# Another order of a graph layer's first loads and last stages, and 358 picked tiles in place of 355

## The chip, the cores and the metric

The kernel runs on one core of a Trainium2 chip. A core has five engines with an instruction queue each, which run side by side and wait for each other by semaphores: TensorE (PE in the profile; its weight loads are PEld), VectorE (DVE), ScalarE (ACT), GpSimd (POOL) and SyncE (SP). SP, ACT and POOL also issue DMA transfers. The metric is the device time of one execution in microseconds; the median of three runs before the change is 1521.2 us (1520.66 to 1521.42). One further execution was profiled.

## The reference, cut to what matters

200,000 edges, sorted by destination, carry messages between 6,250 nodes with 64 features (E edges; `src`, `dst` are node numbers):

```python
w     = silu(edge_attr @ W1 + b1) @ W2 + b2                     # E x 9
h_src = x[src]                                                  # E x 64: a row per edge
msg   = einsum('ef,em,fmg->eg', h_src, edge_sh * w, W_tp)
agg   = segment_sum(msg, dst, 6250) / sqrt(16)
emb   = silu(c_noise[:, None] @ Wn1 + bn1) @ Wn2 + bn2
gamma, beta = split(emb, 2)
out   = layernorm(x + agg * (1 + gamma) + beta)
```

The costly line is `x[src]`: 200,000 rows of 256 bytes in random order.

## The kernel before, in words

**Tiles and groups.** 128 edges are a tile; 16 tiles are a group (`KB`); there are 98 groups (`NBLK`), numbered from 0, of which the last has 11 tiles. The source rows of a group lie in a buffer `hs[g]` (128 x 16 x 64); there are seven such buffers. A row of `x` gets there in one of three ways:

- *Gather* (`gather`, L91): POOL issues an indirect DMA per tile. Group g's gathers stand in POOL's queue six groups ahead (`AHEAD`).
- *Pick* (`pick`, L475 to L486): for the last `picked(g)` tiles of a group, three or four, TensorE multiplies a one-hot matrix with all of `x`, kept in SBUF as two halves `xs[0]`, `xs[1]` (a rounded value and the rest). That is 7 x 2 matmuls into `px`; VectorE masks the result (`xm`, L484) and reduces it into `hs` (L486). The one-hot operands `hot_k` are made by `hots` (VectorE, L460) from keys that stand in every partition (`pk`, copied by ScalarE in `keys` from `kr`, a broadcast load).
- *Direct row loads* (`load_rows`, L106): for every sixth group from 7 on (`SPG`), tile 0 is loaded row by row by SP.

So a group has 16 - `picked(g)` gathers, one fewer if it is in `SPG`. In the kernel before, `picked` is 3 for g mod 8 in {0, 3, 6}, else 4: 355 picks and 1192 gathers.

**Stages of a group.** `hidden` (L403, L411) is the first layer of the edge network with its Silu, `second` (L420) the second, `weights` (L430 to L442) turns the result and multiplies it by `sh` and the one-hot windows `oh` (from `near`, L382) into `a`. `windows` (L504 to L514) sums each tile's messages into windows of 8 nodes: 16 pairs of matmuls of `hs` and `a` into `pz`, which ScalarE copies into `zt`. `project` (L538, L543) multiplies two groups' `zt` by `W_tp`; `turn`, `halves` and `place` (L549, L524 to L528, L559) put the window sums at their nodes; `bring` (L576) and `finish` (L670 to L684) end 128-node blocks with the layer norm and a store.

**Order.** The order is written out by hand: each engine's queue is the order in which the Python code calls. The main loop, for i in 0..97, calls gather(i+6), the loads, `pick(i+1, 0)` with the node stages of i woven between its matmuls, `hidden(i+2)`, `second(i+1)`, `windows(i)`, `project` for odd i, and then picks 1 to 3 of group i+1 (L603 to L651). At the end (i = 96, 97) `windows` came after the picks; then the last projection.

**Setup** (`setup`, L134 to L321) loads the operands, issues the gathers of groups 0 to 5, makes all keys with VectorE (nine passes over 392 columns, L205 to L225), sends them to DRAM and reads them back into every partition (`kd`, `kr`), and splits `x`: ScalarE copies each of seven slices once to PSUM and once, rounded, to `xs[0]`; VectorE subtracts (L294). Then the first picks.

Of the kernel before, what the change touches and what calls it, by code (L numbers as in the profile page):

```python
# [15 lines left out]
P = 128  # L16
N, F, M, D, H, E = 6250, 64, 9, 32, 64, 200000
NJ = 49
# [31 lines left out]
def picked(g):  # L50

    return Q - (3 * g % 8 < 3)
# [7 lines left out]
def gnn_resnorm_kernel(ctx: ExitStack, tc: tile.TileContext, x, src, dst, dst_row, ea, sh, cn,  # L60
# [18 lines left out]
    with ExitStack() as fast:  # L79
# [54 lines left out]
        def setup(temp):  # L134
# [4 lines left out]
            for q in range(4):  # L139
                nc.sync.dma_start(w1bd[q * D:(q + 1) * D, (q % 2) * H:(q % 2 + 1) * H], w1)  # L140
            nc.sync.dma_start(src_i[:, AHEAD * KB:], src[:, AHEAD * KB:])
            xb_r = xb.rearrange("p j f -> p (j f)")
            row_i = xb_r[0:1, 0:NBLK * KB].bitcast(I32)
            nc.scalar.dma_start(row_i, dst[0:1, :])
            first_i = temp.tile([NBLK, KB], I32)
            nc.scalar.dma_start(first_i, dst[0].rearrange("(g k) -> g k", k=KB))
            cn_j = temp.tile([NJ, P], F32)
            nc.scalar.dma_start(cn_j, cn)
            for s in range(2):
                nc.scalar.dma_start(b1c[s * H:(s + 1) * H, :], b1.unsqueeze(1))  # L150
# [3 lines left out]
            for h0, h1 in ((0, 2), (2, 4), (4, 7)):  # L154
                nc.scalar.dma_start(xk[:, h0:h1, :], x_v[:, h0:h1, :])
            load(0)
            for s in range(2):
                nc.sync.dma_start(w2p[s * H:(s + 1) * H, s * M:(s + 1) * M], w2)
            nc.sync.dma_start(dst_i, dst)
# [14 lines left out]
            one = temp.tile([1, 1], F32)  # L174
            nc.vector.memset(one, 0.0)
            one_o = temp.tile([1, 1], F32)
            nc.scalar.activation(one_o, one, AF.Silu)
            row_f = xb_r[0:1, NBLK * KB:2 * NBLK * KB]
            nc.scalar.copy(row_f, row_i)
            first_t = temp.tile([NBLK, KB], F32)  # L180
            nc.scalar.copy(first_t, first_i)
# [5 lines left out]
            nc.vector.tensor_add(ident2, ident[:, 0:F], ident[:, F:P])  # L187
            zero = temp.tile([P, 1], F32)
            nc.vector.memset(zero, 0.0)
            for k in range(2):  # L190
                nc.vector.memset(ht[k][H:H + 1], 1.0)
            nc.vector.memset(wtc2[F:P, 4], 0.0)
            ones1 = temp.tile([1, P], F32)
            nc.vector.memset(ones1, 1.0)
            nc.vector.memset(eps, EPS)
            nc.vector.tensor_copy(nk, nk_i)
            nc.vector.tensor_copy(wi, n_i[:, 0:W])
            nc.vector.tensor_copy(li, n_i[:, 0:J])


            zt_r = zt.rearrange("p a c k w -> p (a c k w)")
            s_f, kp, kh, rest, t0, t1 = [zt_r[:, k * C:(k + 1) * C] for k in range(6)]
            ti = [t.bitcast(I32) for t in (t0, t1)]
            s_f = s_f.rearrange("p (g k) -> p g k", k=Q)
            nc.vector.tensor_copy(s_f[:, 0:NBLK - 1, :],  # L205
                                  src_i.rearrange("p (g k) -> p g k", k=KB)[:, 0:NBLK - 1, KB - Q:])
            nc.vector.tensor_copy(s_f[:, NBLK - 1, :], src_i[:, NT - Q:NT])
            s_f = s_f.rearrange("p g k -> p (g k)")
            nc.vector.tensor_scalar(ti[0], s_f, 2675.0, None, op0=ALU.mult)
            nc.vector.tensor_scalar(ti[0], ti[0], 17, None, op0=ALU.logical_shift_right)  # L210
            nc.vector.tensor_copy(kp, ti[0])
            nc.vector.scalar_tensor_tensor(rest, kp, -float(J * J), s_f, op0=ALU.mult, op1=ALU.add)
            nc.vector.tensor_scalar(ti[1], rest, 37.0, None, op0=ALU.mult)
            nc.vector.tensor_scalar(ti[1], ti[1], 8, None, op0=ALU.logical_shift_right)
            nc.vector.tensor_scalar(kh, ti[1], float(P), None, op0=ALU.mult)
            kf = s_f
            nc.vector.tensor_add(kf, kp, kh)
            for c0 in range(0, C, P):
                n = min(P, C - c0)
                p_kt = psum.tile([P, P], F32, tag=("s", "r")[c0 // P % 2], name=f"p_kt{c0}")  # L220
                nc.tensor.transpose(p_kt[0:n], kf[:, c0:c0 + n], ident)
                kt = t1[:, c0 // 2:c0 // 2 + P // 2].bitcast(F16)
                nc.scalar.copy(kt[0:n], p_kt[0:n])
                nc.sync.dma_start(kd[c0:c0 + n, :], kt[0:n])
            nc.vector.scalar_tensor_tensor(jl, kh, -float(J) / P, rest, op0=ALU.mult, op1=ALU.add)  # L225
            hidden(0, act=False)
            load_keys(0)
            load_keys(LB)
            for c in range(KB // 4):
                for s in range(2):  # L230
                    q = c * D + s * M
                    nc.sync.dma_start(b2c[q:q + M, :], b2.unsqueeze(1))


            rel_v = rel.rearrange("p (a b c) -> p a b c", a=2, b=2)
            dst_v = dst_i.rearrange("p (a b c) -> p a b c", a=2, b=2)
            row_v = row_f.rearrange("p (a b c) -> p a b c", a=2, b=2)

            def base(a_):
                p_b = psum.tile([P, 2, KB * P // 4], F32, tag="p1", name=f"p_b{a_}")  # L240
                for b_ in range(2):
                    nc.tensor.matmul(p_b[:, b_, 0:NBLK * KB // 4], ones1, row_v[:, a_, b_, :], start=True, stop=True)
                nc.vector.tensor_sub(rel_v[:, a_], dst_v[:, a_], p_b[:, :, 0:NBLK * KB // 4])


# [8 lines left out]
            nc.vector.tensor_copy(pw, pw_i)  # L254

            def ids():
                p_nid = psum.tile([P, NBLK], F32, tag="s", name="p_nid")
                nc.tensor.matmul(p_nid, sel, first_f, start=True, stop=True)
                nc.vector.scalar_tensor_tensor(nid, p_nid, pw, lo, op0=ALU.add, op1=ALU.subtract)

            def between(h):

                if h == 0:
                    p_f = psum.tile([KB, NBLK], F32, tag="s", name="p_f")
                    nc.tensor.matmul(p_f, first_t, ident[0:NBLK, 0:NBLK], start=True, stop=True)
                    nc.scalar.copy(first_f, p_f)
                elif h == 1:
                    keys(0)
                    hots(0, 0, Q)
                elif h == 3:  # L270
                    p_cn = psum.tile([P, NJ], F32, tag="s", name="p_cn")
                    nc.tensor.matmul(p_cn, cn_j, ident[0:NJ, 0:NJ], start=True, stop=True)
                    cn_s = temp.tile([P, NJ], F32)
                    nc.scalar.copy(cn_s, p_cn)
                    nc.sync.dma_start(cn_d, cn_s)
                    nc.sync.dma_start(wn1c, wn1.rearrange("o h -> h o"))
                    nc.sync.dma_start(bn1c, bn1.unsqueeze(1))
                    gate_load(0)
                    nc.sync.dma_start(wn2a[0:H, :], wn2)
                    nc.sync.dma_start(wn2a[H:H + 1, :], bn2.unsqueeze(0))  # L280
                    for q in range(2):
                        n = (M + 1 - q) // 2
                        nc.sync.dma_start(wtc2[q * F:(q + 1) * F, 0:n, :], wtp[:, q:M:2, :])
                    load(LB)
                    with nc.allow_non_contiguous_dma(reason="2048 words, once"):
                        nc.sync.dma_start(src_r, src[:, SPG[0] * KB:NBLK * KB:6 * KB].rearrange("p g -> g p"))


            for h in range(J):
                xh = gam[:, h * J:(h + 1) * J, :].rearrange("p l f -> p f l")  # L290
                xp = psum.tile([P, F, J], F32, tag="px" if h in (2, 3) else "pz", name=f"x{h}", bufs=2)
                nc.scalar.copy(xp, xh)
                nc.scalar.copy(xs[0][:, h], xh)
                nc.vector.tensor_sub(xs[1][:, h], xp, xs[0][:, h].bitcast(F32))  # L294
                if h == 1:
                    hidden_act(0)
                between(h)
            pick(0, 0)
            keys(1)
            hots(1, 0, Q)  # L300
            base(0)
            near(0)
            second(0)
            pick(0, 1)
            base(1)

            nc.vector.memset(rel[:, NT:], 0.0)
            if E % P:
                nc.vector.memset(rel[E % P:, NT - 1:NT], 0.0)
            for f in weights(0):  # L310
                f()
            ids()
            hidden(1)
            nc.scalar.copy(zt[F:P, :, 4].rearrange("p a k w -> p a (k w)"),
                           zero[F:P, :, None].to_broadcast([F, 4, P]))
# [543 lines left out]
```

## Time and profile before

| | |
|---|---|
| median of three runs | 1521.2 us |
| the profiled execution's own time | 1521.78 us |
| its span, first to last instruction | 1519.9 us |
| mean granted TensorE clock | 0.983 of full speed |
| PE busy | 1438.0 us (95%) |
| POOL busy | 1129.3 us (74%) |
| VectorE busy | 1135.4 us (75%) |
| ScalarE busy | 526.1 us (35%) |
| gathers (L91) | 1192, 946 ns each |
| pick matmuls (L475) | 4970 recorded, 1090.6 us busy |

What lies around the span is 1521.78 - 1519.9 = 1.88 us. Busy time counts an engine's instructions alone: issuing a DMA or waiting at a semaphore is not busy, and for POOL's gathers some time between two of them is not either. A row of the groups gives line, engine, operation, what it writes and reads, the count, busy time and mean, then the engine's idle time ahead of them and what ended it. The timeline gives start, length, and in brackets the idle time before.

### The profile page before, as it was taken

The page shows a single profiled execution, that of the slowest core. Times are in us where ns is not written, and L with a number is a line of the kernel's source. Part 1 is how long each engine was busy: PE and PEld are TensorE (multiplying, and loading weights), DVE is VectorE, ACT ScalarE, POOL GpSimd, SP SyncE. Part 2 cuts the span into 40 slices and gives each one's busy share as a digit, 9 for nine tenths or more (in the row PEclk, how much of TensorE's full clock was granted, in tenths as well). Part 3 has the DMA queues.
Part 4 walks back from the last instruction along what each step waited for, and adds up shares of the span by engine and source line. Part 5 has one row for each costly group of instructions (what it writes and reads, how often), then busy time and mean ns, then how long its engine had stood idle before and what let it go on. Part 6 is the DMA issues. An engine that isn't in the chain of part 4 may idle for free.

```text
span 1519.9 us, 34363 instructions
## 1 busy us (share of the span) xinstructions
PE 1438.0 (95%) x10810; PEld 1192.7 (78%) x10810; DVE 1135.4 (75%) x1987; ACT 526.1 (35%) x1335; POOL 1129.3 (74%) x1201
## 2 busy tenths in 40 slices
PE   4998999999999999999999999989998998999995
PEld 2787888888888788888888888878777887878784
DVE  5686777877877878777777877768677777687773
ACT  4223342433423333332423424424233333333331
POOL 7777777777777777777777777777777777777772
PEclk9999999999999999999999999999999999999997
DMA  6422232222222222222322222222222222222210
GB/s 171 95 56 63 54 76 53 64 59 70 65 56 72 58 63 71 60 63 54 74 59 55 72 52 63 71 54 61 53 72 53 59 55 71 52 55 59 73 29 15
DMA packets 90939, 96.16 MB, mean 63 GB/s; under 512 B 37161, under 2 KB 51451, under 8 KB 90748
## 3 DMA queue, kind: packets, MB, share of 16 engines
q0 software_dynamic: 38144, 39.14, 13.4%
q1 hardware_dynamic: 51842, 53.09, 12.1%
q8 instruction: 88, 1.44, 0.4%
q10 hardware_dynamic: 762, 1.64, 0.3%
q14 instruction: 103, 0.84, 0.2%
HBM read 92.04 MB, written 1.73 MB: 62 GB/s over the span
## 4 chain that ended last, share of the span: by engine, by line
PE 57%; POOL 18%; issue 9%; SPq 5%; DMA 5%; DVE 4%; ACT 2%; DVEq 0%; POOLq 0%; ACTq 0%
PE px L475 41%; POOL hs L91 18%; PE pz L504 5%; DMA hs<-in_x_dram,src_i 4%; PE p L403 3%; SPq L106 3%; PE pt L543 3%; PE p L420 2%; SPq L101 2%; PE p L430 1%; PE ps L559 1%; PE ps L589 0%; ACT st L411 0%; DVE hot_k L460 0%; DVE xm L484 0%
## 5 line engine op out<-in xcount | busy, mean ns | idle before, releaser
L91 POOL DMA_INDIRECT hs<-in_x_dram,src_i x1192 | 1128.0, 946 | 364.3 <-issue 330.7
L475 PE MATMUL px<-xs,hot_k 128*128 128x448 f32 x4970 | 1090.6, 372 | 9.4 <-DVE xs L294 8.8
L475 PEld LDWEIGHTS px<-xs,hot_k 128*128 128x128 f32 x4970 | 896.8, 189 | 93.9 <-issue 10.9
L484 DVE SCALAR_TENSOR_TENSOR xm<-li,jl,px 128x448 f32<-128x448 f32 x355 | 240.3, 677 | 203.6 <-PE px L475 202.0
L460 DVE TENSOR_TENSOR hot_k<-pk,nk 128x896 fp32r<-128x896 f32 x355 | 370.6, 1082 | 3.1 <-ACT pk L454 3.1
L411 ACT ACTIVATE st<-p,b1c 128x1024 f32<-128x1024 f32 x98 | 109.5, 1118 | 405.4 <-PE p L403 405.1
L486 DVE TENSOR_REDUCE hs<-xm 128x64 f32<-128x448 f32 x355 | 220.1, 620 | 12.2
L514 ACT COPY zt<-pz 64x160 f32<-64x160 f32 (+2 forms) x784 | 213.5, 272 | 40.6 <-PE pz L504 28.0
L504 PEld LDWEIGHTS pz<-a,hs 128*64 128x64 f32 x3126 | 110.2, 142 | 68.1 <-issue 61.2
L504 PE MATMUL pz<-a,hs 128*64 128x72 f32 x3126 | 124.6, 234 | 27.0 <-DMA hs<-in_x_dram,src_i 11.5
L442 DVE TENSOR_TENSOR a<-oh,p 128x1152 f32<-128x1152 f32 x98 | 132.7, 1354 | 3.3
L436 DVE TENSOR_TENSOR p<-p,sh 128x72 f32<-128x72 f32 x196 | 47.0, 240 | 100.9 <-ACT rt L546 45.2
L403 PE MATMUL p<-ea,w1bd 64*128 64x512 f32 x392 | 113.3, 655 | 0.0
L565 ACT COPY carry<-ps 128x128 f32<-128x128 f32 x48 | 12.8, 266 | 273.4 <-PE ps L559 273.4
L420 PEld LDWEIGHTS p<-st,w2p 128*32 128x32 f32 x784 | 15.8, 108 | 83.2 <-issue 39.0
L420 PE MATMUL p<-st,w2p 128*32 128x256 f32 x784 | 63.5, 396 | 7.8 <-DVE xb L356 7.8
L680 ACT ACTIVATE var<-var,eps 128x2 f32<-128x2 f32 (+1 forms) x25 | 7.4, 295 | 179.2 <-DVE var L679 179.2
L543 PE MATMUL pt<-zt,wtc 128*64 128x128 f32 x960 | 64.3, 281 | 2.6 <-ACT zt L514 1.7
L543 PEld LDWEIGHTS pt<-zt,wtc 128*64 128x64 f32 x960 | 55.0, 142 | 3.8 <-ACT zt L514 1.9
L454 ACT CAST pk<-kr 128x384 f32<-128x384 f16 (+1 forms) x98 | 53.8, 549 | 2.2 <-DMA kr<-kd 2.2
L430 PE MATMUL p<-ident,p2s 128*128 128x128 f32 x196 | 53.3, 273 | 0.0
L403 PEld LDWEIGHTS p<-ea,w1bd 64*128 64x128 f32 x392 | 30.0, 187 | 28.7 <-issue 28.0
(122 smaller groups left out, 529.0 us busy)
## 6 DMA issues: line engine op xcount, KB each, us to landing
hs<-in_x_dram SPq DMA_DIRECT2D x2048, 0.2 KB
ea<-in_ea_dram SPq DMA_DIRECT2D x49, 512.0 KB
hs<-in_x_dram,src_i POOLq DMA_INDIRECT x1192
kr<-kd SPq DMA_DIRECT2D x49, 256.0 KB
sh<-in_sh_dram SPq DMA_DIRECT2D x49, 144.0 KB
cb<-cn_d SPq DMA_DIRECT2D x12, 128.0 KB
out_dram<-o SPq DMA_DIRECT2D x24, 64.0 KB
gam<-in_x_dram ACTq DMA_DIRECT2D x2, 448.0 KB
```

Source lines behind the costliest of these rows:

```text
L91: hs_dma[g] = [nc.gpsimd.indirect_dma_start(out=hs[g][:, t - g * KB, :], out_offset=None, in_=x, in_offset=bass.IndirectOffsetOnAxis(ap=sr ...
L403: nc.tensor.matmul(p1[:, i, :], w1bd[i * 64:(i + 1) * 64, :], e[i * 64:(i + 1) * 64, :], start=True, stop=True)
L411: nc.scalar.activation(st[g], p1_t.pop(g), AF.Silu, bias=b1c)
L420: nc.tensor.matmul(p2[g][c * D:(c + 1) * D, 0, :].rearrange("p (i e) -> p i e", i=2), w2p, s[:, :, c * P:(c + 1) * P], start=True, stop=True)
L442: nc.vector.tensor_mul(a[g], oh_t.pop(g)[:, :, None, :].to_broadcast([P, KB, M, W]), sw.unsqueeze(3).to_broadcast([P, KB, M, W]))
L460: nc.vector.tensor_tensor(hot_k[g, t], pk_t[g][:, t, None, :].to_broadcast([P, J, P]), nk.unsqueeze(2).to_broadcast([P, J, P]), op=ALU.is_ ...
L475: nc.tensor.matmul(px.rearrange("p f l -> p (f l)"), hot_k[g, t][:, h, :], xs[i][:, h].rearrange("p f l -> p (f l)"), start=(h == 0 and i ...
L484: nc.vector.scalar_tensor_tensor(xm, li[:, None, :].to_broadcast([P, F, J]), jl[:, c:c + 1], px, op0=ALU.is_equal, op1=ALU.mult)
L486: nc.vector.tensor_reduce(hs[g][:, tiles(g) - q + t, :], xm, AX.X, ALU.add)
L504: mm = nc.tensor.matmul(pz[v * F:(v + 1) * F, k // 2].rearrange("p m w -> p (m w)"), hsg[:, k0 + k, :], ag[:, k0 + k].rearrange("p m w -> ...
L514: nc.scalar.copy(z[h * F:(h + 1) * F, 0:5 - h, k0 + v:k0 + n:2, :].rearrange("p m k w -> p k m w"), pz[v * F:(v + 1) * F, 0:(n + 1 - v) // ...
L543: nc.tensor.matmul(pt[h * F:(h + 1) * F, 0, 0:P], wtc2[:, c, :], z[h][:, c], start=(c == 0), stop=(c == 4))
```

## The change

- `picked` is 3 for g mod 3 = 0 and for the last group, else 4: 358 picks, 1189 gathers. The last group has 3 picks and 7 gathers where it had 4 and 6.
- Setup: ScalarE's queue issues only the loads of `x`, ahead of everything; SP's queue has the rest in the order of first use (the source indices stay SP's first). Keys of groups 0 and 1 alone are made first; they are spread over the partitions by a matmul of ones with a diagonal matrix (`keys_first`) in place of the way through DRAM; the other groups' keys follow later (`keys_rest`). `x` is split from SBUF: ScalarE copies once, VectorE subtracts with both operands in SBUF. The first layer of group 0 comes behind the first pick. The first node of each tile, `row_i`, is loaded by DMA into every partition, so that `rel` is a subtraction of two SBUF operands in place of matmuls of ones and a subtraction from PSUM.
- End: `windows(96)` stands behind the first pick of group 97, with `project(48)` between picks and `place` behind the last; `bring` of blocks 46 and 47 comes before `windows(97)`, whose second half is done first and whose copies are shared by ScalarE and VectorE. PSUM tags change.
- Stores are issued by a list that the next iteration empties. In SP's queue they stand where they stood.

The diff, cut:

```diff
 def picked(g):
-    return Q - (3 * g % 8 < 3)
+    return Q - (g % 3 == 0 or g == NBLK - 1)
...
+            x_v = x.rearrange("(p h l) f -> p h (l f)", h=J, l=J)
+            for h0, h1 in ((0, 1), (1, 2), (2, 4), (4, 7)):
+                nc.scalar.dma_start(xk[:, h0:h1, :], x_v[:, h0:h1, :])
...
+            load(0, split=True)
+            nc.sync.dma_start(dst_i[:, 0:2 * KB], dst[:, 0:2 * KB])
+            nc.sync.dma_start(row_i[:, 0:2 * KB], rows(dst[0, 0:2 * KB], P))
...
+            def keys_first(g, kf, tag):
+                pk_t[g] = psum.tile([P, Q, P], F32, tag=tag, name=f"pk{g}")
+                for t in range(picked(g)):
...
+                    nc.vector.tensor_scalar(dg, ident, kf[:, c:c + 1], None, op0=ALU.mult)
+                    nc.tensor.matmul(pk_t[g][:, t, :], ones, dg, start=True, stop=True)
...
+            def split(h):
+                xh = gam[:, h * J:(h + 1) * J, :].rearrange("p l f -> p f l")
+                nc.scalar.copy(xs[0][:, h], xh)
+                nc.vector.tensor_sub(xs[1][:, h], xh, xs[0][:, h].bitcast(F32))
+            kf = keys_of(0, LB)
+            keys_first(0, kf, "r")
+            hots(0, 0, 1)
+            for h in range(J):
+                split(h)
+                if h == J // 2:
+                    hots(0, 1, 2)
...
+            pick(0, 0)
+            hots(0, 2, Q)
+            hidden(0)
+            keys_first(1, kf, "s")
...
+            nc.sync.dma_start(dst_i[:, 2 * KB:], dst[:, 2 * KB:])
+            nc.sync.dma_start(row_i[:, 2 * KB:], rows(dst[0, 2 * KB:], P))
+            load(LB)
+            keys_rest(keys_of(LB, NBLK))
+            load_keys(LB)
...
+            nc.vector.tensor_sub(rel[:, 2 * KB:], dst_i[:, 2 * KB:], row_i[:, 2 * KB:])
...
-            for h in range(J):
-                xh = gam[:, h * J:(h + 1) * J, :].rearrange("p l f -> p f l")
-                xp = psum.tile([P, F, J], F32, tag="px" if h in (2, 3) else "pz", name=f"x{h}", bufs=2)
-                nc.scalar.copy(xp, xh)
-                nc.scalar.copy(xs[0][:, h], xh)
-                nc.vector.tensor_sub(xs[1][:, h], xp, xs[0][:, h].bitcast(F32))
...
+            end = g == NBLK - 1
+            for k0 in reversed(range(0, nk, ZT)) if end else range(0, nk, ZT):
...
-                        nc.scalar.copy(
+                        (nc.vector.tensor_copy if end and v else nc.scalar.copy)(
...
-                if i < NBLK - 2:
+                if i < NBLK - 1:
                     windows(i)
-                turn = project(i // 2) if i % 2 == 1 else []
+                turn = project(i // 2) if i % 2 == 1 and i < NBLK - 1 else []
...
+                if i == NBLK - 2:
+                    sums(i + 1)
+                    turn = project(i // 2)
+                    ps = psum.tile([P, 2 * P], F32, tag="s", name="ps_l")
+                    pick(i + 1, 2, [turn])
+                    more = place(i // 2, ps)
...
+            for f in bring(NJ - 3, NJ - 1, psum.tile([P, FB, F], F32, tag="s", name="py_l")):
+                f()
+            windows(NBLK - 1)
             project(NBLK // 2)
```

## The prediction

> **What bounds the kernel now.** I read the page first, then POOL's waits and timeline, then TensorE's timeline at the first, middle and last groups.
>
> ```profile
> PE 1438.0 (95%) x10810; PEld 1192.7 (78%) x10810; DVE 1135.4 (75%) x1987; ACT 526.1 (35%) x1335; POOL 1129.3 (74%) x1201
> ...
> PE 57%; POOL 18%; issue 9%; SPq 5%; DMA 5%; DVE 4%; ACT 2%; DVEq 0%; POOLq 0%; ACTq 0%
> ```
>
> Busy time and the chain both point at TensorE. The waits say otherwise:
>
> ```profile
> POOL hs L91 <- issue: 330.7, 1084, 0.3
> ```
>
> POOL is idle only 0.3 us at a time, 1084 times, before a gather, with nothing to wait for. Its timeline begins and ends so:
>
> ```profile
> 2.92 1.11 POOL L91 DMA_INDIRECT hs<-in_x_dram,src_i  x1 [0.97 <-DMA src_i<-in_src_dram]
> ...
> 1493.22 0.94 POOL L91 DMA_INDIRECT hs<-in_x_dram,src_i  x1 [0.30 <-issue]
> ```
>
> 1192 gathers start between 2.92 and 1493.22: (1493.22 - 2.92) / 1191 = 1.2513 us each, and no gap between two starts is over 1.61 us. POOL never waits for a buffer; it sets the pace from the first gather to the last.
>
> TensorE starts late and catches up. Group 6's last gather starts at 110.95; a matmul that waits for a gather starts 2.6 us after the gather's start where TensorE stood idle for it (1363.1 to 1365.7 in group 88). So the rows were there at 113.6, but the window matmuls start at 149.78: TensorE is 36.2 us behind. In group 62 (965.26 and 967.81) it is 0.0 behind: it gained 36.2 / 56 = 0.65 us a group. From there on it waits for gathers; the windows view of the stretches up to there, behind it, and of the end:
>
> ```profile
> 55.80:967.80 912.00, 897.70 (x6863) 749.11 (x6859) 710.61 (x1251) 321.40 (x830) 689.47 (x730) 1.00 0.26 62
> 967.80:1493.70 525.90, 499.59 (x3757) 417.04 (x3753) 386.14 (x642) 176.24 (x452) 397.73 (x421) 0.99 0.24 58
> 1493.70:1519.90 26.20, 10.16 (x95) 8.30 (x94) 7.64 (x28) 6.85 (x23) 0.47 (x1) 0.62 0.04 9
> ```
>
> PE busy (second number) falls from 98% of the stretch to 95%, while POOL keeps its rate. The end is a chain of short steps, from TensorE's timeline:
>
> ```profile
> 1485.71 8.08 PE L475 MATMUL px<-xs,hot_k 128*128 128x448 f32 x38
> 1493.72 1.22 PE L504 MATMUL pz<-a,hs 128*64 128x72 f32 x32
> ...
> 1502.01 1.67 PE L504 MATMUL pz<-a,hs 128*64 128x72 f32 x22
> 1506.35 2.40 PE L538 MATMUL pt<-wtc,zt 128*128 128x64 f32 x10 [2.67 <-ACT zt L514]
> ```
>
> Group 96's rows (last gather 1485.7, there at 1488.3) wait 5.4 us for group 97's picks, and group 97's (there at 1495.8) wait until 1502.01.
>
> **What the Trainium skill says.** "SBUF — State Buffer", Who interferes with whom: VectorE and GpSimd share a port pair under an exclusive lock, and a VectorE instruction with two SBUF inputs contends with a GpSimd instruction that reads SBUF. The trace agrees: the one gather of 1.30 us in the setup stands beside an addition of two SBUF operands.
>
> ```profile
> 11.76 0.57 DVE L217 TENSOR_TENSOR zt<-zt 128x392 f32<-128x392 f32 x1
> 11.84 1.30 POOL L91 DMA_INDIRECT hs<-in_x_dram,src_i  x1 [0.30 <-issue]
> ```
>
> It ends at 12.33, 0.49 after the gather's start, and the gather is 0.36 longer than the usual 0.94. At 1425.53 a gather takes 1.20 beside `oh` (L382, ends 0.37 after the start; 0.26 longer). So the lengthening is what is left of the VectorE operation less 0.13. Subtractions with one operand in PSUM (L294, seven of 0.62) lengthened no gather. "TensorE: Matmul & The Clock Gate", Part 1: after an idle window of about 3.4 us the clock is halved. Agreed: behind 4.39 us of idleness up to 1168.76, the clock is 0.50 over 1168.7 to 1172.1. "DMA: Bandwidth & Descriptors", Anatomy of one DMA — SWDGE, gives about 2.0 us fixed per DMA; the 2.6 above is used.
>
> **The change part by part.** All against the profiled span of 1519.9.
>
> *Gathers.* 1192 - 1189 = 3 fewer: 3 x 1.2513 = **-3.75** for the last gather.
>
> *First gather.* The indices stay SP's first transfer, but the first slice of x (224 KB) is now on ScalarE's queue beside them. At 305 GB/s, the most that the windows of the start show, that is 0.7 us; it delays between 0 and 1.2. I take **+0.3**.
>
> *Locks at the start.* The split of x now has both operands in SBUF: 7 x 0.62 us. If the gather's reading point falls anywhere in 1.25, an operation of length d costs d x d / (2 x 1.25) on average: 0.154, seven 1.1. `rel` is 1536 columns from SBUF in one piece; by L243 (784 columns, 0.97) and L217 (392, 0.57) a column is 1.03 ns with 0.16 fixed: 1.75 us, longer than a period, so it hits one gather, by 1.75 - 0.63 = 1.1. The key passes stay as wide in sum. Sum **+2.2**, between 0 (all miss, `rel` aside 0.5) and 4.5. Nothing covers it: what a gather loses all later gathers lose.
>
> *TensorE's start.* First picks: before, pick 0 ended at 31.98, behind keys through DRAM and 14 copies of 0.92 to 0.95. Now seven copies (6.7) follow x, which lands between some 3 and 8: about 12.5. Part is given back: TensorE waits for the other keys, made only behind group 0's third pick at some 25 (nine passes 4.5, three transposes with copies 2.9, DRAM write and read 4.6 and 3.7, as the chain has them): `kr` of group 2 lands near 41, and ScalarE's copy, with `hidden` and `weights` behind it, and VectorE's `hots`, with the masks behind it, queue up. `windows(1)`, 70.2 before, comes at about 59: 11 us earlier (5 to 16). SP's new order puts nothing ahead of what POOL needs. This is worth **0** in time: POOL covers it. It matters only as lead.
>
> *Three picks more.* 14 x 0.20 = 2.81 us each on TensorE. The starts of `windows` lie, while TensorE is the bound, 13.3 (3 picks, even group), 13.1 (3, odd), 14.7 (4, odd), 16.1 (4, even) apart (166.1, 179.4, 194.1, 210.2, 223.3). Six groups now: 13.3 + 14.7 + 16.1 + 13.1 + 16.1 + 14.7 = 88.0; POOL: 73 x 1.2513 = 91.3. The lead per group is 0.55; the same sum for before gives 14.50 against 14.63 seen, so I take 0.42. From 36.2 - 11 = 25 behind at group 6, level at about group 66. With no earlier start it is group 92: just in time. **0**.
>
> *Stores, PSUM tags.* In SP's queue the stores stand where they were: 0. `py_l` now shares a bank with `ps_l` and so waits for both its readers; it is in the next sum.
>
> *The end.* Last gather: 1493.22 - 3.75 + 0.3 + 2.2 = 1491.97. Group 96's is seven earlier, 1483.2; `windows(96)` at 1485.8, TensorE waiting for it some 3 us (12 us of work since `windows(95)`, 16.3 of gathers). Behind it: windows 1.2; pick with two transposes 3.3 (4.5); `project` 1.25 (5.75); pick and turn 3.0 (8.75); mask and reduction 0.07 + 1.33 (10.15), behind which VectorE adds `yt`, 0.3 (10.45); `bring` 0.55 (11.0); the norm to `var` 2.2, Sqrt 0.3 (13.5), VectorE's last two 0.55 (14.05). ScalarE's four copies follow Sqrt, VectorE's four follow its own: 0.9 (14.95; a copy from PSUM by VectorE is not in the trace; 0.29 by the like of L568). The last window matmuls (their gathers there at 8.8) lie under the norm. From the start of the last projection to the end the trace has 1519.9 - 1506.35 = 13.55: 15.05 + 13.55 = 28.6. The wait before `windows(96)` is long enough to halve the clock: 1.7 us, in four of the six waits over 2.2 seen: **+1.2**. Sum 29.8; 1485.8 + 29.8 = **1515.6**, against 1519.9: -4.3. Between 27.5 and 31.5 for the end.
>
> The profiled time is 1.88 above its span, the median 0.58 below that: **1516.9 us**.
>
> **The rivals.**
>
> *A, TensorE is the bound throughout*, as the chain has it. Then the earlier start counts, -11, the picks +8.4, the end -3.5 (28.6 less 8.75 behind the last pick, against 26.1, and 2.8 now ahead of it): 1515.1. Nearly the same time, but group 96's rows would lie waiting. Against: POOL's 1084 waits of 0.3. 0.04.
>
> *B, the end gives nothing*: TensorE reaches `windows(96)` late, or VectorE's queue holds the copies. POOL's -1.25 is left: 1520.0. For: the end is many short steps with estimates between them. 0.20.
>
> *C, slower: the lock holds each gather for the whole of every two-operand pass at the start.* Seven splits 4.3, `rel` 1.75, key passes some 4.5: 10.6 in place of 2.2, so 1525.3. It decides from 9.5 us of lost gather time. Against: nine key passes before lost 0.36. 0.08.
>
> *D, the locks miss and the clock stays whole*: 1516.9 - 2.2 - 1.2 = 1513.5. 0.13.
>
> **How the numbers follow.** My forecast, 1514.5 to 1518.2, has 0.55. A measurement of this kernel tells 0.2% (3.0 us) from no change: under 1518.2 is faster, over 1524.2 slower. Faster: 0.55 + 0.04 + 0.13 = 0.72; same 0.20; slower 0.08. The range takes in D with an undelayed first gather (1513.2) and a shorter end (27.5 for 28.6), and most of B: 1512 to 1521.
>
> **What would show it.** Right: 1189 gathers without a wait; their last start near 1492; lengthened gathers at the seven L235 subtractions and the L309 one; TensorE level with POOL near group 66, idle before `windows(96)`; about 30 us from there to the end. Wrong: POOL waiting for a buffer, `windows(96)` starting over 4 us after its rows, a later first gather than 4.1, or lost gather time beyond 4.5 us.

## The result, and the profile after

The changed kernel takes 1518.39 us (median of 13 runs, 1516.86 to 1520.27) against 1520.66 us (13 runs, 1519.88 to 1521.42): ratio 0.9985, 95% interval 0.9976 to 0.9994. It is 2.3 us faster, which is less than the 3.0 us that the prediction asked for to call it faster. Its profiled execution took 1520.27 us, the longest of the 13, with a span of 1518.5 (clock 0.981). So 1.4 us separate the two spans, and 2.3 the two medians.

The page of the changed kernel, busy time and the chain, and then POOL's waits (time in all, how often, longest):

```profile
PE 1445.6 (95%) x10857; PEld 1201.2 (79%) x10857; DVE 1150.1 (76%) x2017; ACT 518.4 (34%) x1321; POOL 1130.1 (74%) x1198
...
PE 70%; POOL 13%; issue 6%; DVE 6%; DMA 4%; ACT 1%; SPq 0%; DVEq 0%; POOLq 0%; ACTq 0%
```

```profile
POOL hs L91 <- issue: 332.2, 1089, 0.3
...
POOL hs L91 <- DMA src_i<-in_src_dram: 1.9, 1, 1.9
```

The chain points at TensorE even more than before (70% for 57%), and POOL still waits 0.3 us between gathers for nothing. POOL's timeline, the first gather, the longest one and the last:

```profile
3.88 1.11 POOL L91 DMA_INDIRECT hs<-in_x_dram,src_i  x1 [1.93 <-DMA src_i<-in_src_dram]
...
48.48 2.06 POOL L91 DMA_INDIRECT hs<-in_x_dram,src_i  x1 [0.30 <-issue]
...
1494.19 0.95 POOL L91 DMA_INDIRECT hs<-in_x_dram,src_i  x1 [0.30 <-issue]
```

The last gather starts 0.97 us *later* than before (1493.22), with three gathers fewer. The starts of all gathers say why. I take a period (start to start) under 1262 ns as undisturbed and add up what the others have beyond the mean of those:

| | before | changed | difference |
|---|---|---|---|
| first gather starts | 2.92 | 3.88 | +0.96 |
| three gathers fewer | 1192 | 1189 | -3.75 |
| lengthened periods in the first 60 us | 0.66 | 3.21 | +2.55 |
| lengthened periods later | 2.45 | 1.02 | -1.43 |
| undisturbed period | 1248.7 ns | 1250.9 ns | +2.63 over 1188 |
| last gather starts | 1493.22 | 1494.19 | +0.97 |
| from there to the end | 26.68 | 24.31 | -2.37 |

The fifth line is not the change's: of the seven versions below that are made from the changed kernel, six have 1248.6 to 1248.8 ns, and five of these have all its gathers and picks. What sets it stays open (see the end).

TensorE's timeline at the end, and the windows view of the same three kinds of stretch as before (second number PE busy, then further engines, the granted clock third from the end):

```profile
1483.91 0.64 PE L419 MATMUL p<-st,w2p 128*32 128x256 f32 x8
1488.15 1.87 PE L507 MATMUL pz<-a,hs 128*64 128x72 f32 x32 [3.59 <-DMA hs<-in_x_dram,src_i]
...
1494.10 1.31 PE L547 MATMUL pt<-zt,wtc 128*64 128x128 f32 x20
...
1505.06 2.37 PE L541 MATMUL pr<-wtc,zt 128*128 128x64 f32 x10 [3.35 <-DVE zt L517]
```

```profile
53.30:988.00 934.70, 919.88 (x7050) 768.25 (x7047) 731.65 (x1282) 330.81 (x850) 706.89 (x747) 1.00 0.25 64
988.00:1488.15 500.15, 479.27 (x3580) 400.01 (x3580) 370.84 (x615) 166.88 (x432) 378.29 (x400) 0.98 0.23 58
1488.15:1518.50 30.35, 15.78 (x124) 13.40 (x124) 11.70 (x37) 5.93 (x19) 5.46 (x6) 0.68 0.06 14
```

TensorE counts as level at the first group whose windows start within 0.5 us of its rows (2.6 us after the start of its last gather). As forecast, that is group 66 here, and TensorE stands idle for 3.59 us before `windows(96)`. The windows then take 1.87 us for 1.22, and the pick behind them 4.15 (1489.95 to 1494.10), at half clock; 30.35 us lie between their start and the end.

### The profile page after: what moved, and what is told of

Read it like the earlier page. It is cut to its first block, busy times and chain, and to the rows that moved or that the text cites. A ratio compares the mean times of both kernels' runs of the same rounds, so it can differ in the third digit from the quotient of the medians.

```text
span 1518.5 us, 34473 instructions
## 1 busy us (share of the span) xinstructions
PE 1445.6 (95%) x10857; PEld 1201.2 (79%) x10857; DVE 1150.1 (76%) x2017; ACT 518.4 (34%) x1321; POOL 1130.1 (74%) x1198
## 4 chain that ended last, share of the span: by engine, by line
PE 70%; POOL 13%; issue 6%; DVE 6%; DMA 4%; ACT 1%; SPq 0%; DVEq 0%; POOLq 0%; ACTq 0%
PE px L474 51%; POOL hs L91 13%; PE pz L507 6%; PE p L402 4%; DMA hs<-in_x_dram,src_i 3%; PE pt L547 3%; PE p L419 3%; PE p L429 1%; PE ps L593 1%; PE ps L563 1%; DVE xm L483 1%; DVE hs L485 0%; DVE hot_k L459 0%; ACT L410 0%; ACT var L688 0%
## 5 line engine op out<-in xcount | busy, mean ns | idle before, releaser
L474 PE MATMUL px<-xs,hot_k 128*128 128x448 f32 x5012 | 1105.3, 374 | 2.0 <-ACT xs L234 1.3
L474 PEld LDWEIGHTS px<-xs,hot_k 128*128 128x128 f32 x5012 | 907.2, 190 | 87.3 <-issue 9.4
L459 DVE TENSOR_TENSOR hot_k<-pk,nk 128x896 fp32r<-128x896 f32 x358 | 373.5, 1080 | 1.9 <-PE pk L220 1.9
L517 ACT COPY zt<-pz 64x160 f32<-64x160 f32 (+1 forms) x780 | 212.6, 273 | 28.0 <-PE pz L507 19.5
L419 PE MATMUL p<-st,w2p 128*32 128x256 f32 x784 | 63.5, 396 | 12.5 <-DVE xb L351 7.9
L453 ACT CAST pk<-kr 128x512 f32<-128x512 f16 (+1 forms) x96 | 53.0, 552 | 0.0
L402 PEld LDWEIGHTS p<-ea,w1bd 64*128 64x128 f32 x392 | 29.8, 186 | 29.1 <-issue 28.5
```

What stands on the lines that cost most here:

```text
L402: nc.tensor.matmul(p1[:, i, :], w1bd[i * 64:(i + 1) * 64, :], e[i * 64:(i + 1) * 64, :], start=True, stop=True)
L419: nc.tensor.matmul(p2[g][c * D:(c + 1) * D, 0, :].rearrange("p (i e) -> p i e", i=2), w2p, s[:, :, c * P:(c + 1) * P], start=True, stop=True)
L459: nc.vector.tensor_tensor(hot_k[g, t], pk_t[g][:, t, None, :].to_broadcast([P, J, P]), nk.unsqueeze(2).to_broadcast([P, J, P]), op=ALU.is_ ...
L474: nc.tensor.matmul(px.rearrange("p f l -> p (f l)"), hot_k[g, t][:, h, :], xs[i][:, h].rearrange("p f l -> p (f l)"), start=(h == 0 and i ...
L517: (nc.vector.tensor_copy if end and v else nc.scalar.copy)(z[h * F:(h + 1) * F, 0:5 - h, k0 + v:k0 + n:2, :].rearrange("p m k w -> p k m w ...
```

## The experiments

Each was timed beside the kernel before on the same chip; differences are to the median of those runs of before (1520.85 to 1521.25), so that the changed kernel stands at -2.3. Where the 95% intervals of two versions overlap, the times alone don't tell them apart, and the text says so. In short:

| | us | to before | ratio, 95% |
|---|---|---|---|
| before, picks alone | 1513.71 | -7.2 | 0.9950 (0.9937 to 0.9964) |
| before, last group alone | 1518.06 | -2.8 | 0.9982 (0.9975 to 0.9989) |
| before, picks and end | 1514.94 | -5.9 | 0.9958 (0.9945 to 0.9972) |
| changed, picks back | 1527.08 | +6.1 | 1.0037 (1.0024 to 1.0051) |
| changed, end back | 1517.72 | -3.2 | 0.9977 (0.9968 to 0.9986) |
| changed, second pick first | 1516.63 | -4.3 | 0.9972 (0.9964 to 0.9981) |
| changed, start from PSUM | 1515.64 | -5.6 | 0.9960 (0.9947 to 0.9974) |
| changed, small loads ahead of x | 1518.14 | -3.1 | 0.9979 (0.9973 to 0.9986) |
| changed, other buffer for keys | 1518.57 | -2.7 | 0.9983 (0.9975 to 0.9991) |
| put together | 1507.64 | -13.6 | 0.9913 (0.9900 to 0.9927) |

### The picks

```diff
 def picked(g):
-    return Q - (3 * g % 8 < 3)
+    return Q - (g % 3 == 0 or g == NBLK - 1)
```

in the kernel before:

> The kernel before with the changed picked alone (358 picks, the last group 3 picks and 7 gathers). Theory, POOL's gathers set the time: up to group 95 four gathers are saved (4 x 1.25 = -5.0 us), and group 97's picks, behind which the old order puts the last windows, are one fewer (-2.8 us): -7.8 us if TensorE has caught up by group 95 (by the forecast's sum it has at group 92), so 1513 us, lower than the whole change. Rival, a gather saved is worth its 1.25 us and nothing else: -3.75. Rival, TensorE is the bound throughout: +8.4. Rival, TensorE has not caught up: between -7.8 and 0, with no idle time of PE before windows(95).

Measured: 1513.71 us, -7.2. The same line taken back in the changed kernel:

> The changed kernel with the old picked (355 picks, the last group 4 picks and 6 gathers). Theory: group 96's rows come four gathers later (+5.0 us) and one more pick stands between windows(96) and the end (+2.8): +7.8 us against the changed kernel, near 1526. Rival, 1.25 us per gather alone: +3.75. Rival, TensorE is the bound: -8.4.

Measured: 1527.08 us, 8.4 above the changed kernel (each against its own runs of before). More matmuls make the kernel faster and fewer make it slower, both by the size that POOL's gathers and the last group give; TensorE as the bound has the wrong sign twice. And one line of the change, alone, brings three times what the whole change brings. How much of it is the last group was asked of the kernel before with

```diff
-    return Q - (3 * g % 8 < 3)
+    return Q - (3 * g % 8 < 3 or g == NBLK - 1)
```

> The kernel before with three picks in the last group in place of four, and nothing else: one pick fewer (354), one gather more (1193). Theory: no gather up to group 96 moves, and a pick goes from the path between group 95's rows and the end: -2.8 us, though POOL's last gather starts 1.25 us later. Rival, POOL's last gather sets the end: +1.25. Rival, the picks of the last group are hidden: 0.

Measured: 1518.06 us, -2.8. In its profiled execution POOL's last gather starts at 1494.03, 0.8 later than before, and the span is 2.0 shorter. TensorE's timeline, last group:

```profile
1486.95 5.05 PE L475 MATMUL px<-xs,hot_k 128*128 128x448 f32 x24
1491.93 1.22 PE L504 MATMUL pz<-a,hs 128*64 128x72 f32 x32
...
1500.17 1.67 PE L504 MATMUL pz<-a,hs 128*64 128x72 f32 x22 [0.20 <-PE py_l L576]
```

A row of 24 pick matmuls where the kernel before had 38, and all behind it sooner: before, `windows(96)` started at 1493.72 and `windows(97)` at 1502.01. What sets the end is not POOL's last gather but the rows that TensorE last waited for, those of an earlier group (95 in the kernel before, with 0.41 us of idle time), with the picks that TensorE does behind them. The rest of the -7.2, 4.4, is near the four gathers that stand less ahead of group 96 (5.0).

### The end

The changed order added to the picks, in the kernel before (the parts of the diff in the main loop from `if i < NBLK - 1`, in `windows` and in `project`):

> The kernel before with two parts of the change: picked, and the order, copies and PSUM buffers of the last two groups; its loads, keys and split stay as they were. Theory: the new order of the end is worth nothing or a little less (from the last gather of group 96 to the end 33.1 us in the changed kernel, 31.9 with the picks alone): 0 to +1.2 us against the run with picked alone (1513.7), so near 1514.4, and the start is what takes the rest back (3.5 to 4 us). Rival, the end costs most of the 4.7 us that the change loses against its picks alone: near 1518. Rival, the end gains 3 as forecast: near 1510.7.

Measured: 1514.94 us, -5.9, 1.3 more than the picks alone. The two intervals overlap, but the traces agree with it: the time from the last gather to the end goes from 23.1 (1491.27 to 1514.4) to 24.4 (1488.77 to 1513.2). TensorE's timeline, the picks alone and then with the new order:

```profile
1483.33 5.05 PE L475 MATMUL px<-xs,hot_k 128*128 128x448 f32 x24
1488.31 1.22 PE L504 MATMUL pz<-a,hs 128*64 128x72 f32 x32
```

```profile
1482.83 1.92 PE L506 MATMUL pz<-a,hs 128*64 128x72 f32 x32 [3.18 <-DMA hs<-in_x_dram,src_i]
```

In the first, picks fill the time in which the second waits. The converse, the old order in the changed kernel (and with it copies by ScalarE alone, the halves of `windows(97)` in their old order and the old PSUM buffers; `bring` of blocks 46 and 47 stands ahead of `windows(97)` in both kernels):

```diff
-                if i < NBLK - 1:
+                if i < NBLK - 2:
                     windows(i)
...
+                if i >= NBLK - 2:
+                    windows(i)
```

> The changed kernel with the old order of its last two groups (all picks of group 97 ahead of windows(96), bring of blocks 46 and 47 ahead of windows(97), copies by ScalarE alone, old PSUM buffers); loads, keys, split and picks as changed. The forecast's step on the end: the new order gains 28.6 + 1.2 against 26.2 with 5.4 + 2.8 us of picks ahead, so undoing it costs +3 or more. Theory now: in the changed kernel PE stands idle 3.6 us before windows(96) and then does two picks behind it, at half clock at first; in the old order both picks (5.6 us) run in that idle time, windows(96) starts 2 us later and 26.2 us remain in place of 30.3: -2.1 us. Rival, the end sets nothing: 0.

Measured: 1517.72 us, -3.2, 0.9 better than the changed kernel. The intervals of the two ratios overlap, so the time alone does not tell this one from no effect; from the last gather to the end its trace has 23.6 us for 24.3. It is not the forecast's gain of 3. Added or taken away, the new order costs about 1 us, each time by the medians and by the trace. TensorE's timeline of this run:

```profile
1484.59 5.18 PE L474 MATMUL px<-xs,hot_k 128*128 128x448 f32 x24
1489.70 1.22 PE L507 MATMUL pz<-a,hs 128*64 128x72 f32 x32
...
1498.28 1.67 PE L507 MATMUL pz<-a,hs 128*64 128x72 f32 x22 [0.19 <-PE py_l L581]
```

There is no bracket ahead of `windows(96)`: the picks fill the wait for the rows, and the clock stays whole (1.22 for 1.87). `windows(96)` starts 3.3 us behind its rows (last gather of group 96 at 1492.50 - 7 x 1.25 = 1483.75, and 2.6), not the 2 that I expected, so the gain was smaller than 2.1. Between the two orders lies this one:

```diff
                     second(i + 1)
+                if i == NBLK - 2:
+                    pick(i + 1, 1, [weights(i + 1)])
                 if i < NBLK - 1:
                     windows(i)
...
-                if i + 1 < NBLK:
+                if i + 1 < NBLK - 1:
                     pick(i + 1, 1, [weights(i + 1), turn])
```

> The changed kernel with one step moved: windows(96) behind the second pick of group 97, not the first. Theory: the pick (2.8 us) fills the idle 3.6 us, the clock isn't halved, windows(96) starts as before; 4.15 us of pick and 0.65 of slow windows go, but project now waits some 2.2 us for ScalarE's copies of zt: -2.4 us (between -1.5 and -4.0; beyond -4.0 group 97's gathers would bound windows(97)). Rival, what waits is group 97's rows or VectorE's queue: 0.

Measured: 1516.63 us, -4.3, 2.0 better than the changed kernel. These two intervals overlap as well; from the last gather to the end the trace has 22.6 us for 24.3. The timeline:

```profile
1485.30 2.25 PE L474 MATMUL px<-xs,hot_k 128*128 128x448 f32 x10
1487.48 1.22 PE L507 MATMUL pz<-a,hs 128*64 128x72 f32 x32
1488.53 0.38 PE L547 MATMUL pt<-zt,wtc 128*64 128x128 f32 x2
1490.56 1.30 PE L547 MATMUL pt<-zt,wtc 128*64 128x128 f32 x18 [1.65 <-ACT zt L517]
```

One pick in the idle time, no half clock, and the wait for ScalarE's copies, which the pick had covered, is there at 1.65 us.

### The start

The two kinds of passes with two SBUF operands undone:

```diff
+                xp = psum.tile([P, F, J], F32, tag="px" if h in (2, 3) else "pz", name=f"x{h}", bufs=2)
+                nc.scalar.copy(xp, xh)
                 nc.scalar.copy(xs[0][:, h], xh)
-                nc.vector.tensor_sub(xs[1][:, h], xh, xs[0][:, h].bitcast(F32))
+                nc.vector.tensor_sub(xs[1][:, h], xp, xs[0][:, h].bitcast(F32))
...
-            nc.vector.tensor_sub(rel[:, 2 * KB:], dst_i[:, 2 * KB:], row_i[:, 2 * KB:])
+            for c0, n, tag in ((2 * KB, 2, "p1"), (2 * KB + 1024, 1, "r")):
+                p_r = psum.tile([P, n, 512], F32, tag=tag, name=f"p_r{c0}")
+                c1 = c0 + n * 512
+                nc.scalar.copy(p_r.rearrange("p a n -> p (a n)"), row_i[:, c0:c1])
+                nc.vector.tensor_sub(rel[:, c0:c1], dst_i[:, c0:c1], p_r.rearrange("p a n -> p (a n)"))
```

> The changed kernel with the two kinds of two-SBUF-operand passes of its start undone: ScalarE copies each slice of x to PSUM as well, as before, and VectorE subtracts from there; the row of first nodes is copied to PSUM in two pieces and rel is subtracted from there. Theory, the lock on the port that VectorE and POOL share: the four gathers beside the splits (1.47 us too long in all) and the one beside rel (1.12) become normal: -2.6 us, with TensorE's first pick some 6 us later at no cost. Rival, the start of POOL's gathers is lengthened by something else of the start (the loads' traffic): 0. Rival, TensorE's start counts: +4 or more.

Measured: 1515.64 us, -5.6, 3.3 better than the changed kernel, with an interval apart from its own, although TensorE's first pick ends 2.4 us later (18.8 for 16.4) and `windows(1)` starts at 70.19 for 67.72 there. The lengthened periods of the first 60 us fall from 3.21 to 0.93. The two kernels beside each other, VectorE and POOL (timeline):

```profile
47.97 1.75 DVE L309 TENSOR_TENSOR rel<-dst_i,xb 128x1536 f32<-128x1536 int32 x1
48.48 2.06 POOL L91 DMA_INDIRECT hs<-in_x_dram,src_i  x1 [0.30 <-issue]
```

```profile
37.95 0.36 DVE L201 TENSOR_SCALAR zt<-zt 128x384 int32<-128x384 f32 x1
37.99 1.13 POOL L91 DMA_INDIRECT hs<-in_x_dram,src_i  x1 [0.31 <-issue]
...
50.69 1.22 DVE L315 TENSOR_TENSOR rel<-dst_i,p_r 128x1024 f32<-128x1024 int32 x1
51.82 0.68 DVE L315 TENSOR_TENSOR rel<-dst_i,p_r 128x512 f32<-128x512 int32 x1
```

In the changed kernel `rel` ends at 49.72, 1.24 behind the gather's start, and the gather is 1.12 too long: what is left of the pass, less 0.13, as the prediction had it. With the operand from PSUM there is no long gather beside `rel` at all, nor beside any of the seven splits. Nor is it VectorE's work as such that counts: in the changed kernel a `hot_k` pass (L459, with `pk` in PSUM) stands over the same moment, 0.13 us behind the start, of 307 gathers, and none of these is longer by more than 0.01 us. This is what the Trainium skill's "SBUF — State Buffer", Who interferes with whom, says of two SBUF inputs; the 1.13 beside the key pass L201, with *one* SBUF operand, fits its remark that such operations, too, can take the shared pair in a mode with two ports.

The loads of `first_i`, `cn_j` and `b1c` moved from SP's queue to ScalarE's, ahead of `x`:

```diff
+            nc.scalar.dma_start(first_i, dst[0].rearrange("(g k) -> g k", k=KB))
...
+            nc.scalar.dma_start(cn_j, cn)
+            for s in range(2):
+                nc.scalar.dma_start(b1c[s * H:(s + 1) * H, :], b1.unsqueeze(1))
             for h0, h1 in ((0, 1), (1, 2), (2, 4), (4, 7)):
```

> The changed kernel with four small loads (first_i, cn_j, b1c twice) ahead of x in ScalarE's queue, as before the change, and so no longer in SP's. Theory, the first slice of x delays the source indices: the first gather starts at 2.9 to 3.1 instead of 3.9 and everything behind it is that much earlier: -0.9 us. Rival, the indices are late because of the order in SP's queue or the descriptors, which stay: 0.

Measured: 1518.14 us, -3.1: 0.8 better by the medians, with overlapping intervals. The trace shows the cause of the late first gather. The queues of the changed kernel, then the one that moved, and POOL's first gather, here:

```profile
0.75 3.21 ACTq L143 DMA_DIRECT2D gam<-in_x_dram  x4
0.76 0.42 SPq L138 DMA_DIRECT2D src_i<-in_src_dram  x1
...
6.75 1.43 SPq L152 DMA_DIRECT2D b1c<-in_b_dram  x2
```

```profile
0.76 0.42 SPq L138 DMA_DIRECT2D src_i<-in_src_dram  x1
...
2.95 3.90 ACTq L149 DMA_DIRECT2D gam<-in_x_dram  x4
...
3.01 1.11 POOL L91 DMA_INDIRECT hs<-in_x_dram,src_i  x1 [1.06 <-DMA src_i<-in_src_dram]
```

SP issues the indices at 0.76 in both, and the loads taken from its queue stood at 6.75 and later, behind the first gather; what is no longer beside the indices is `x`, issued at 2.95 and not at 0.75. The gather starts 0.87 earlier, but `x` and the splits come later against the gathers and hit them worse: the lengthened periods of the start are 3.86 for 3.21. By the trace 0.2 of the 0.9 is kept.

The keys of group 1 in another PSUM buffer:

```diff
-            keys_first(1, kf, "s")
+            keys_first(1, kf, "pz")
```

(with two buffers for that tag).

> The changed kernel with the keys of group 1 in a window buffer (pz) of PSUM instead of the one that second(0) needs. Theory: second(0), which waits 4.9 us for the last reader of those keys, starts some 4 us earlier, windows(0) and windows(1) up to as much, TensorE is level with POOL some 5 groups sooner, and the time is the same (0), since POOL's gathers set it. Rival, TensorE's start counts: -4.

Measured: 1518.57 us, -2.7, the same as the changed kernel. TensorE's timeline, first the changed kernel, then this one:

```profile
27.70 1.08 PE L419 MATMUL p<-st,w2p 128*32 128x256 f32 x8 [4.58 <-issue]
```

```profile
24.85 0.64 PE L419 MATMUL p<-st,w2p 128*32 128x256 f32 x8
```

`second(0)` now comes behind the pick that stood after it, with no wait, 2.85 us earlier; `windows(0)` starts at 51.33 for 53.30 (55.9 to 56.4 in the profiles of three other versions with the changed start), and TensorE is level at group 63. An earlier TensorE is worth nothing at this end of the kernel.

### What the findings give together

```diff
-    return Q - (g % 3 == 0 or g == NBLK - 1)
+    return Q - (g % 3 == 0 and g not in (30, 36, 42, 48, 54) or g == NBLK - 1)
```

with `rel` from PSUM, the small loads ahead of `x`, the other buffer for the keys, and the second pick first:

> A version put together from the findings: the changed kernel with rel from PSUM (-1.1), the small loads ahead of x (-0.9), the keys of group 1 in a window buffer (0, some 4 us of lead), windows(96) behind the second pick (-1.8, by the trace of that run alone) and a fourth pick in groups 30, 36, 42, 48 and 54 (363 picks, 1184 gathers: 5 x 1.25 = -6.25; 14 us of TensorE's lead of about 17): -10.0 us, near 1508.4. Rival, TensorE isn't level by group 96: up to -3 only, with no idle time before the last windows.

Measured: 1507.64 us, -13.6 and 0.9913 of the kernel before: faster than both kernels, and 11.3 below the changed one where 10.0 was expected. The parts were not timed one by one here. TensorE now is level at group 90 only, and reaches `windows(96)` with no idle time:

```profile
1477.74 2.25 PE L478 MATMUL px<-xs,hot_k 128*128 128x448 f32 x10
1479.93 1.22 PE L511 MATMUL pz<-a,hs 128*64 128x72 f32 x32
```

The lead that an earlier TensorE gives is worth something once picks are bought with it.

## Why the prediction was right, and where it was not

1516.9 was forecast and 1518.39 measured, inside the range. As a gain that is 2.3 us where 4.3 were forecast (from 1521.2), about half; the chances leaned too far to "faster by over 0.2%" (0.72), and 0.15% came.

**What bounds the kernel** was right: POOL sets the pace, whatever the chain says, shown from both sides by the picks. Rival A, TensorE the bound throughout, is out. Rival C, the lock for whole passes, is out: 2.55 us were lost at the start and not 10.6. Rival D is out, too: the locks hit and the clock fell. Rival B's time, 1520.0, did not come, and the time behind the last gather did fall; but of the order itself B is nearer the truth than the forecast, since the experiments put that fall down to the last group's pick and not to the order.

**Gathers** (-3.75): right, as a sum. For the end, the four gathers that go from ahead of group 96 are what counts.

**First gather**: +0.3 forecast, +0.96 measured, and the cause, `x` beside the indices, shown by the version with small loads ahead.

**Locks at the start**: +2.2 forecast, +2.55 measured. The mechanism was right, and each term: `rel` 1.1 forecast and 1.12 measured, the splits 1.1 and 1.47. A split took 0.93 us and not 0.62, the duration from PSUM: the step took its price from a row with another operand. And its formula left out the 0.13 that it had found itself. With both put right it gives 7 x 0.80 x 0.80 / 2.5 = 1.8. The same four of seven hit in all five profiles with this order of loads (1.43 to 1.47 in all); where `x` comes later, four hit with 1.97 (small loads ahead of `x`) and two with 1.00 (put together).

**TensorE's start**: `windows(1)` was to come 11 us earlier and came 2.5 earlier in this profile (67.72 for 70.17). Even that is not the change's: three other profiles with the same start (picks back, end back, second pick first) have 70.3 to 71.1, and the four with the old start 68.4 to 70.6. So the step's gain did not come. The end of the first pick is at 16.4 and not 12.5, and a PSUM buffer that the step had not looked at (the keys of group 1 in the one that `second(0)` needs) held TensorE for 4.6 us, of which the version with the other buffer got 2.0 back at `windows(0)`. The passes over the other keys began at 35.0 and not at some 25. That TensorE's start is worth 0 held: with the start from PSUM `windows(1)` came no earlier than before the change and the time fell; with the other buffer it came earlier and the time stayed.

**Three picks more**: level at group 66, as forecast, by two errors that cancel (and in this profile; end back and second pick first, with the same start and picks, are level at 72 and 69). TensorE was 29.0 us behind at group 6 and not 25, and gained 29.0 / 60 = 0.48 us a group and not 0.42. With no earlier start (the picks alone) it is level at group 69, where the step said 92, "just in time": it gains (33.8 at group 6) / 63 = 0.54 there. The sum of the step had 0.55, and the step trimmed it to 0.42.

**The end**: 29.8 us from the start of `windows(96)` forecast and 30.35 measured, the wait and the half clock as described. (The step's sum slips by 0.1, from 14.95 to 15.05.) This is the step that was right for the wrong reason. It compared the new order with the old end as profiled, which has *four* picks in the last group, and so could not see that the gain is the fourth pick's (-2.8 alone) and that the new order costs about 1. Moving `windows(96)` to where its rows are not yet there left the pick behind it on the path.

The last sums: first gather 0.66 more than forecast, locks 0.35 and the end 0.55, together 1.56. The profiled span is 2.9 above the forecast's 1515.6. Nearly all of it is these 1.56 and another 1.20: 2.63 more of undisturbed period less 1.43 of lengthened periods later, for which the forecast had no term and which no run ties to the change. That the median, too, is 1.5 above its forecast is in part luck: the forecast started from 1521.2, and the 13 runs of before have 1520.66.

The gain of the picks alone, 7.2 us, so went, by the medians: 1.3 to the order of the end, and the rest, 3.6, to the start, where the traces show 3.5 (0.96 + 2.55).

## What to carry to other kernels

Where one queue paces a kernel from its first instruction to its last, everything in the setup is priced by what it does to that queue alone: 1 us of late indices or of a held port stays to the end, while three more picks, 8.4 us of the busiest engine, cost nothing. Ahead of a wait, put work that doesn't need what is awaited, and price a new order of the end against the old order with the same amounts of work, not against the profile as it stands. Lead on the engine that is not the bound is worth what can be bought with it, here a gather (1.25 us) for each 2.8 us of TensorE.

## What was not expected of the hardware

- The undisturbed period of the gathers has two values, constant through an execution: 1250.7 to 1250.9 ns in three of twelve profiled executions (the changed kernel, the picks alone, the picks back) and 1248.6 to 1248.8 in the other nine. Over 1189 gathers that is 2.5 us, as much as the whole change. What decides it stays open; nothing points to the change, as kernels of both values differ by a few lines behind the start.
- TensorE's clock was halved at once behind a wait of 2.68 us (start from PSUM: `windows(96)` 2.19 us, clock 0.50 over it), less than the window of about 3.4 us in the Trainium skill, "TensorE: Matmul & The Clock Gate", Part 1. Behind 3.22 us (small loads ahead of `x`) the windows took 1.35 at a clock of 0.87, and the 2.8 us *after* them ran at 0.50. That page also says that the window runs freely, and the traces agree: from 200 us on, all 51 stretches at half clock in the twelve profiles begin on a grid of 3.413 us (in the kernel before at 1090.19, 1168.70, 1291.58 and 1411.05: 23, 36 and 35 steps apart). What went with the half clock is how long TensorE stood idle within one step of that grid: each of the 50 stretches up to 1508 us follows a step with 1.66 us or more of idleness, and no step after which the clock stayed whole has more than 1.88. So of the 2.68 us above, 2.51 lie in the step that ends at 1483.88, just before the windows; and 2.98 us of idleness up to 999.21 in the kernel before, of which 1.80 and 1.18 lie in two steps, halved nothing. So a plan should reckon with about half a step of idleness, wherever the grid falls, and not with a whole one.
- A split, a subtraction of two SBUF operands of 128 x 448, took 0.93 us, and with one of them in PSUM 0.62. Two operands in SBUF do not cost that by themselves: `rel`, with 1536 columns, took 1.75, the prediction's 1.03 ns a column and 0.16, which would be 0.62 for a split. The split also reads `x` in steps of 64 numbers, and the version from PSUM has ScalarE do that; that the step is what costs was not tested alone.
